# Folding a gate through Wo: column quarters of 32 with 512 columns moving, placed between two batches' query transposes

## The chip, the cores and the metric

The kernel runs on one core of a Trainium2 chip. The metric is the device time of one execution in microseconds, as the median of several runs. All tensors are fp32.

## The reference, cut to what matters

Two layers, each x + FFN(cond(x)), for x of 8 x 256 tokens and 512 features. Layer 0's cond is attention over a paged key-value cache with a window of 256; its FFN routes each token to 2 of 8 experts by a gate. What the change touches is the end of attention and the gate:

```python
o = o.transpose(0, 2, 1, 3).reshape(Bx, Tx, H * HD)
return jnp.einsum('bto,do->btd', o, Wo)          # output of attention
...
logits = jnp.clip(xt @ gate_w.T, -50.0, 50.0)    # xt: that output, gate_w: 8 x 512
top_w, top_idx = jax.lax.top_k(logits, TOP_K)
```

The logits are o Wo^T gate_w^T. The kernel therefore computes the product Wo^T gate_w^T (512 x 8) once, calls it gwo, and multiplies each batch's o by it, so that the routing need not wait for the attention's output rows.

## The kernel before, in words

The program is one long list that a scheduler puts in order on each engine: it follows the order of the code, its own estimate of times, and the buffers of the pools. Only `in_a_row` and `keep_in_program_order` fix an order by hand. [...]

Stages around the change:

- *Projection* (`with proj:`). 16 row blocks of 128 tokens get their keys and values (`keys_values`), which are written to kv_new in DRAM. Beside it, `base_weights` spreads the base weight of layer 0's FFN into delta_d, and `sum_same` and `add_delta` add sparse updates to it by indirect DMA from the GpSimd queue (six of them, BESIDE, in this stage). `gather_new(0)` gathers the new keys and values of batch 0 from kv_new on the same queue. `later(woT, ...)` and `later(gw, ...)` load Wo^T and the gate on the SP queue at row block 8.
- *Queries of batches 0 and 1*, in the same stage: for each batch `query_rows` (PE: pq, four matmuls for each 128 rows; DVE: rotation into qr; ACT: squares) and then `queries_turned` (PE: four transposes pt for each row block; ACT: copy to QT). The PSUM pools are psq and psd, three buffers each, and pw0 and pw1 are two more banks of psd.
- *The fold.* After `proj` is closed, and ahead of `prepared(0, ...)` in the code, woT is transposed in four column blocks (pw), copied by ACT to won, and for each block four matmuls with won as the stationary side and the gate's 8 columns moving add to four accumulators pgo in PSUM; four ACT copies put them in gwo. It uses the PSUM pools ps_s and ps_o, which attention uses afterwards.
- *Attention*, over batches b and halves t of 128 queries: `prepared` turns the keys of the next batch (PE: pk; DVE: KT, posb, mask), `queries(b + 2)` projects queries two batches ahead (pq from xb), `attend` makes the scores (PE: ps), masks them and takes their maximum (DVE: s<-ps,mask), exponentiates (ACT), transposes (PE: pp) and multiplies with the values (PE: po). `find_rows` (DVE: t, which, m, win, has, old) finds the rows that a later batch gathers. `gate_rows` uses gwo at the end of each batch; it is the first reader of gwo.

Of the kernel before, what the change touches and what calls it, by code (L numbers as in the profile page):

```python
# [11 lines left out]
F32 = mybir.dt.float32  # L12
I32 = mybir.dt.int32
AF = mybir.ActivationFunctionType
ALU = mybir.AluOpType
AX = mybir.AxisListType
# [3 lines left out]
P = 128  # L20
B, T, D = 8, 256, 512
# [3 lines left out]
KC = D // P  # L25
# [6 lines left out]
E = 8  # L32
# [50 lines left out]
def two_layer_kernel(ctx: ExitStack, tc: tile.TileContext, io: dict, out: bass.AP):  # L83
    nc = tc.nc
# [14 lines left out]
    ident = const.tile([P, P], F32, name="ident")  # L99
# [4 lines left out]
    RK, BW = 16, 32  # L104
# [3 lines left out]
    def in_a_row(products):  # L108

        for j, product in enumerate(products):  # L110
            if j == 0:
                product()
            else:
                with tc.high_priority():
                    tc.keep_in_program_order(product())

# [400 lines left out]
    def multiplied(py, xT, weights, experts):  # L519

        if len(experts) == 1:
            for k in range(KC):
                nc.tensor.matmul(  # L523
                    py,
                    xT[:, k, :],
                    of_expert(experts[0])(weights(k)),
                    start=(k == 0),
                    stop=(k == KC - 1),
                )
            return  # L530
        in_a_row(
            lambda k=k, h=h: nc.tensor.matmul(  # L532
                py[h * HR : (h + 1) * HR, :],
                xT[:, k, h * HR : (h + 1) * HR],
                of_expert(experts[h])(weights(k)),
                start=(k == 0),
                stop=(k == KC - 1),
            )
            for k in range(KC)
            for h in (1, 0)  # L540
        )
# [34 lines left out]
    woT = op.tile([P, KC, D], F32, name="woT")  # L576
    gwo = op.tile([P, KC, E], F32, name="gwo")
# [44 lines left out]
    with ExitStack() as att:  # L622
        ap = att.enter_context(tc.tile_pool(name="ap", bufs=1))
# [14 lines left out]
        blocks = [  # L638
            dp.tile([P, KC, 512], F32, name=f"xb{j}", tag="xb", bufs=2) for j in range(NTB + 1)
        ]  # L640
        minus_half = ap.tile([P, 1], F32, name="minus_half")
        nc.gpsimd.memset(minus_half, -0.5)

        gw = ap.tile([P, KC, E], F32, name="gw")
        epss = ap.tile([P, 2], F32, name="epss")
        nc.gpsimd.memset(epss[:, 0:1], EPS)
        nc.gpsimd.memset(epss[:, 1:2], EPS / (SCALE * SCALE))
# [380 lines left out]
        def gather_new(b):  # L1028

            gather(b, kv_new, idx_new, N)  # L1030
# [37 lines left out]
        def query_rows(i, xcols, psum, tag, pool, early=False):  # L1068

            pq = psum.tile([P, H * HD], F32, name="pq", tag=tag)  # L1070
            for k in range(KC):
                nc.tensor.matmul(  # L1072
                    pq, xcols[:, k, :], wq[:, k, :], start=(k == 0), stop=(k == KC - 1)
                )
            q3 = pq.rearrange("p (h d) -> p h d", d=HD)
            qr = pool.tile([P, H, HD], F32, name="qr")
            rotated(i, H, q3, qcos, qsin, qr, pool)
            ms = squares(q3, H, pool)
            by, eps = 1.0 / (HD * SCALE * SCALE), epss[:, 1:2]
            if early:  # L1080
                nc.scalar.activation(ms, ms, AF.Sqrt, bias=eps, scale=by)
                nc.vector.reciprocal(roots[:, i, :], ms)
            else:
                nc.vector.tensor_scalar(ms, ms, by, eps, ALU.mult, ALU.add)
                nc.gpsimd.tensor_tensor(
                    roots[:, i, :], ms, minus_half.to_broadcast([P, H]), ALU.pow
                )
            return qr

        def queries_turned(qrs, psum, tag):  # L1090

            QT = qtp.tile([P, KC, T], F32, name="QT")
            for t, qr in enumerate(qrs):
                qflat = qr.rearrange("p h d -> p (h d)")
                pt = psum.tile([P, KC, P], F32, name="pt", tag=tag)
                for m in range(KC):
                    nc.tensor.transpose(
                        pt[:, m, :], qflat[:, m * P : (m + 1) * P], ident
                    )
                nc.scalar.copy(QT[:, :, t * P : (t + 1) * P], pt)  # L1100
            return QT
# [21 lines left out]
        with proj:  # L1123
# [3 lines left out]
            psd = proj.enter_context(tc.tile_pool(name="psd", bufs=3, space=PSUM))  # L1127
# [52 lines left out]
            for i in range(LEAD):  # L1180
# [11 lines left out]
            pw = [  # L1192
                psd.tile([P, 2, NSQ, E], F32, name=f"pw{h}", tag=f"pw{h}", bufs=1)
                for h in range(2)
            ]
            for j in range(2):
                for k in range(NSQ):
                    for h in range(2):
                        rows = slice(h * ATOMS, (h + 1) * ATOMS)
# [4 lines left out]
                            start=True,  # L1204
                            stop=True,
# [77 lines left out]
            def later(tile, src, rs):  # L1283

                nc.scalar.copy(tile[:, 0, :1], rs[:, :1])
                nc.sync.dma_start(tile, src)

            FIRST = 8
            summed = placed = 0
            for i in range(LEAD, NT):  # L1290
                rs = keys_values(i)
                if i == LEAD:
                    with_gains(qcos, qsin, "q_scale")
                    rot.close()
                base_weights(i)
                if i == 3:
                    later(wq, wsrc[:, :, :512], rs)
                if i == 8:
                    later(woT, io["woT"].rearrange("(c p) o -> p c o", p=P), rs)
                    later(gw, io["gate0T"].rearrange("(c p) e -> p c e", p=P), rs)  # L1300
                if i == 4:
                    find_blocks(psd, rs)
                if i in (6, 8, 10):
                    find_rows(i // 2 - 3)
                if i in (9, 11):
                    gather_old(i // 2 - 4)
                for k in range(summed, min(summed + 3, NSC)):
                    sum_same(k)
                    summed = k + 1
                if summed - placed >= 8 or i == NT - 1:  # L1310
                    find_places(range(placed, summed))
                    placed = summed
                if i >= FIRST and i - FIRST < BESIDE:
                    add_delta(i - FIRST, sums[:, i - FIRST, :])
            gather_new(0)

            qq = proj.enter_context(tc.tile_pool(name="qq", bufs=2, side="right"))
            QTs = {}
            for b in range(2):
                rows = [  # L1320
                    query_rows(
                        i, blocks[NTB][:, :, i * P : (i + 1) * P], psq, "pkv", qq, early=True
                    )
                    for i in range(2 * b, 2 * b + 2)
                ]
                QTs[b] = queries_turned(rows, psd, "psd")


        otp = ost.enter_context(tc.tile_pool(name="otp", bufs=1, side="right"))
# [5 lines left out]
        ps_s = att.enter_context(tc.tile_pool(name="ps_s", bufs=2, space=PSUM))  # L1335
        ps_p = att.enter_context(tc.tile_pool(name="ps_p", bufs=2, space=PSUM))
        ps_o = att.enter_context(tc.tile_pool(name="ps_o", bufs=2, space=PSUM))
# [38 lines left out]
        def attend(b, t, kvs, QT, KT, mask, beside):  # L1376
            oT = oTs[b]
            for m in range(KC):
                u = m // 2

                ps = ps_s.tile([P, 2, 512], F32, name="ps")
                pss = [ps[:, r, :WU] for r in range(2)]
                in_a_row(
                    lambda r=r: nc.tensor.matmul(  # L1384
                        pss[r],
# [38 lines left out]
                for r in range(2):  # L1424
# [3 lines left out]
                    for c in range(3):  # L1428
# [6 lines left out]
                po = ps_o.tile([P, P], F32, name="po", tag="misc")  # L1435
                v0 = G * HD + 2 * u * HD
                in_a_row(
                    lambda c=c, r=r: nc.tensor.matmul(  # L1438
                        po[r * HD : (r + 1) * HD, :],
# [22 lines left out]
            nc.vector.tensor_scalar(lg0[:, i, :], pg, 50.0, -50.0, ALU.min, ALU.max)  # L1462

        AHEAD = 2

        with ExitStack() as fold:
            fo = fold.enter_context(tc.tile_pool(name="fo", bufs=1))
            pgos = [ps_s.tile([P, 2, 512], F32, name="pgo", tag="ps") for j in range(KC // 2)]
            pgo = [pgos[k // 2][:, k % 2, :E] for k in range(KC)]
            for d in range(KC):  # L1470
                pw = ps_o.tile([P, KC, P], F32, name="pw", tag="misc")
                for k in range(KC):
                    nc.tensor.transpose(pw[:, k, :], woT[:, k, d * P : (d + 1) * P], ident)
                won = fo.tile([P, D], F32, name="won")
                nc.scalar.copy(won, pw.rearrange("p c r -> p (c r)"))
                for k in range(KC):
                    nc.tensor.matmul(
                        pgo[k],
                        won[:, k * P : (k + 1) * P],
                        gw[:, d, :],  # L1480
                        start=(d == 0),
                        stop=(d == KC - 1),
                    )
            for k in range(KC):
                nc.scalar.copy(gwo[:, k, :], pgo[k])

        gather_new(1)
        ready = prepared(0, kv_rows[0])
        zero = wop.tile([P, D], F32, name="zero")
# [289 lines left out]
    with ExitStack() as cond:  # L1779
# [3 lines left out]
        with tc.tile_pool(name="ps_g", bufs=1, space=PSUM) as ps_g:  # L1783
            gwc = xab.tile([P, KC, E], F32, name="gwc", bufs=1)
            banks = [(ps_t, "pt"), (ps_g, "misc"), (ps_l, "route_a"), (ps_l, "route_b")]
# [304 lines left out]
```

## Time and profile before

| | us |
|---|---|
| median of 3 runs | 991.62 |
| lowest and highest run | 988.88, 998.61 |
| the profiled execution, as timed | 993.23 |
| its span in the profile | 991.5 |
| fold on PE (first pw to last pgo) | 107.6 to 119.1 |
| first scores on PE (ps) | 129.26 |

The page gives busy times by engine: PE is TensorE's matmuls, PEld its weight loads, DVE VectorE, ACT ScalarE, POOL GpSimd, SP the queue that issues most loads. PEclk is the clock that TensorE was granted as a share of the full one. Matmuls overlap, so the busy time of PE also holds their latency: the pitch of a group is its total time less one latency over its number less one. An fp32 matmul leaves two records, a transpose leaves one. A row of the timeline shows the start, the time, the engine, the line, what is written from what, the number of records, and in brackets the idle time before and what ended it.

### The profile page before, as it was taken

The page shows a single profiled execution, that of the slowest core. Times are in us where ns is not written, and L with a number is a line of the kernel's source. Part 1 is how long each engine was busy: PE and PEld are TensorE (multiplying, and loading weights), DVE is VectorE, ACT ScalarE, POOL GpSimd, SP SyncE. Part 2 cuts the span into 40 slices and gives each one's busy share as a digit, 9 for nine tenths or more (in the row PEclk, how much of TensorE's full clock was granted, in tenths as well). Part 3 has the DMA queues.
Part 4 walks back from the last instruction along what each step waited for, and adds up shares of the span by engine and source line. Part 5 has one row for each costly group of instructions (what it writes and reads, how often), then busy time and mean ns, then how long its engine had stood idle before and what let it go on. Part 6 is the DMA issues. An engine that isn't in the chain of part 4 may idle for free. (4 is left out here: it accounts for less than half of the span.)

```text
span 991.5 us, 14493 instructions
## 1 busy us (share of the span) xinstructions
PE 924.4 (93%) x4917; PEld 524.8 (53%) x4917; DVE 451.3 (46%) x1479; ACT 371.7 (37%) x958; POOL 356.8 (36%) x332
## 2 busy tenths in 40 slices
PE   6999889999999998897999997999599999999995
PEld 3555645556556465564433335545287777753332
DVE  5788698855846766472211112371012322323332
ACT  3676256646647589531111112410111111113221
POOL 2631646565364100305666640000223333333211
PEclk9899699999999999798999995899799999999998
DMA  6697493332432112528997655881434344333222
GB/s 190 224 315 255 133 317 107 99 97 66 138 75 76 43 44 65 190 78 310 338 258 134 127 87 160 305 311 53 170 66 73 64 76 74 64 74 63 51 29 32
DMA packets 74245, 134.71 MB, mean 136 GB/s; under 512 B 17309, under 2 KB 22941, under 8 KB 74032
## 3 DMA queue, kind: packets, MB, share of 16 engines
q0 software_dynamic: 25088, 43.68, 22.6%
q1 hardware_dynamic: 38496, 74.57, 21.7%
q10 hardware_dynamic: 10576, 15.39, 4.2%
q8 instruction: 44, 0.72, 0.3%
q14 instruction: 41, 0.34, 0.1%
HBM read 89.95 MB, written 52.56 MB: 144 GB/s over the span
## 5 line engine op out<-in xcount | busy, mean ns | idle before, releaser
L509 POOL DMA_INDIRECT xs<-g_d,token_i_l x34 | 35.2, 1035 | 241.7 <-PE pa L545 125.8
L551 DVE COPY xsT<-pa 128x512 f32<-128x512 f32 x68 | 46.8, 689 | 154.9 <-PE pa L545 150.0
L1982 DVE TENSOR_TENSOR y<-py,b 64x512 f32<-64x512 f32 (+1 forms) x46 | 31.7, 690 | 185.9 <-PE py L523 122.2
L1966 ACT ACTIVATE hs<-pu,b 128x64 f32<-128x64 f32 (+1 forms) x184 | 46.0, 347 | 186.6 <-PE pu L1940 145.2
L532 PE MATMUL py<-delta,xsT 128*64 128x512 f32 (+1 forms) x416 | 94.8, 599 | 0.0
L1415 ACT ACTIVATE s<-s,mx,roots 128x384 f32<-128x384 f32 x128 | 89.7, 704 | 12.2 <-DVE mx L1411 11.3
L1940 PE MATMUL pu<-xsT,w 128*128 128x128 f32 x704 | 84.1, 279 | 0.0
L1940 PEld LDWEIGHTS pu<-xsT,w 128*128 128x128 f32 x704 | 82.2, 196 | 0.4 <-issue 0.4
L523 PE MATMUL py<-w,hs 128*128 128x512 f32 x176 | 79.3, 594 | 0.0
L556 POOL DMA_INDIRECT out<-y,token_i_l x34 | 53.9, 1586 | 55.7 <-DVE y L1983 55.4
L1438 PE MATMUL po<-pT,kv 128*64 128x128 f32 x768 | 66.7, 285 | 7.1 <-ACT pT L1433 7.1
L1134 PE MATMUL pkv<-wkv,xb 128*128 128x512 f32 x128 | 64.6, 630 | 8.6 <-DMA wkv<-wqkvT 8.3
L1399 DVE CUSTOM_DVE_ANT_0 s<-ps,mask 128x384 f32<-128x384 f32 x128 | 67.2, 551 | 11.5 <-PE ps L1384 10.0
L1757 ACT ACTIVATE y<-py,weight_l 128x512 f32<-128x512 f32 x34 | 23.4, 687 | 125.0 <-PE py L532 89.8
L1438 PEld LDWEIGHTS po<-pT,kv 128*64 128x64 f32 x768 | 46.6, 137 | 42.9 <-ACT pT L1433 35.6
L556 POOL DMA_INDIRECT sums_d<-y,token_i_l x34 | 53.9, 1585 | 32.4 <-ACT y L1757 13.5
L1429 PE MATMUL pp<-ident,s 128*128 128x128 f32 x384 | 59.5, 282 | 3.1 <-DVE s L1426 3.1
L1384 PE MATMUL ps<-KT,QT 64*128 64x384 f32 x256 | 58.1, 533 | 4.3 <-DVE mx L1399 4.2
L1433 ACT COPY pT<-pp 128x384 f32<-128x384 f32 x128 | 55.8, 477 | 16.0 <-PE pp L1429 15.1
L545 PEld LDWEIGHTS pa<-ident,xs 128*128 128x128 f32 x272 | 32.7, 145 | 52.5 <-issue 45.9
L610 PE MATMUL ph<-woT,oT 128*128 128x512 f32 x128 | 60.3, 621 | 0.3 <-DVE lg L1462 0.3
L1072 PE MATMUL pq<-wq,xb 128*128 128x512 f32 x128 | 60.1, 618 | 0.0
(381 smaller groups left out, 1549.7 us busy)
## 6 DMA issues: line engine op xcount, KB each, us to landing
delta_d<-spread SPq DMA_DIRECT2D x16, 512.0 KB, 4.4
raw<-delta_d SPq DMA_DIRECT2D x16, 512.0 KB, 4.6
w<-fc_w SPq DMA_DIRECT2D x8, 1024.0 KB, 20.5
w<-fc_w SPq DMA_DIRECT2D x16, 512.0 KB, 14.3
part<-sums_d SPq DMA_DIRECT2D x32, 256.0 KB, 5.0
xb<-xT SPq DMA_DIRECT2D x5, 1024.0 KB, 6.3
sums_d<-zero SPq DMA_DIRECT2D x18, 256.0 KB, 4.6
kv_new<-kvt ACTq DMA_DIRECT2D x16, 256.0 KB, 3.6
```

The costliest lines, as they stand in the source:

```text
L523: nc.tensor.matmul(py, xT[:, k, :], of_expert(experts[0])(weights(k)), start=(k == 0), stop=(k == KC - 1),)
L532: lambda k=k, h=h: nc.tensor.matmul(py[h * HR : (h + 1) * HR, :], xT[:, k, h * HR : (h + 1) * HR], of_expert(experts[h])(weights(k)), star ...
L556: nc.gpsimd.indirect_dma_start(out=sum_d, out_offset=bass.IndirectOffsetOnAxis(ap=token_i[:, s : s + 1], axis=0), in_=y, in_offset=None, b ...
L610: nc.tensor.matmul(ph, oTs[i // 2][:, k, (i % 2) * P : (i % 2 + 1) * P], woT[:, k, :], start=(k == 0), stop=(k == KC - 1),)
L1072: nc.tensor.matmul(pq, xcols[:, k, :], wq[:, k, :], start=(k == 0), stop=(k == KC - 1))
L1134: nc.tensor.matmul(pkv, xb[:, k, cols], wkv[:, k, :], start=(k == 0), stop=(k == KC - 1),)
L1384: lambda r=r: nc.tensor.matmul(pss[r], QT[r * HD : (r + 1) * HD, m, t * P : (t + 1) * P], KT[r * HD : (r + 1) * HD, u, t * P : t * P + WU] ...
L1399: nc.vector.tensor_tensor_reduce(out=s, in0=pss[r], in1=mask[:, t, :], scale=1.0, scalar=NEG, op0=ALU.add, op1=ALU.max, accum_out=mx[:, r ...
L1415: nc.scalar.activation(ss[r], ss[r], AF.Exp, bias=mx[:, r : r + 1], scale=root[:, r : r + 1], accum_out=sm[:, r : r + 1],)
L1429: nc.tensor.transpose(pp[:, c * P : (c + 1) * P], s[:, c * P : (c + 1) * P], ident)
L1438: lambda c=c, r=r: nc.tensor.matmul(po[r * HD : (r + 1) * HD, :], kvs[t + c][:, v0 + r * HD : v0 + (r + 1) * HD], pTs[r][:, c * P : (c + 1 ...
L1940: nc.tensor.matmul(pu[:, c, :], w1[:, k, plan.full[s], c * P : (c + 1) * P], xsT[:, k, :], start=(k == 0), stop=(k == KC - 1),)
```

## The change

The fold moves into the projection stage, between the query rows of batch 1 and their transposes. It becomes the function `seen_through`. The gate is kept in a tile of 32 columns for each block of 128 rows of Wo's output side, cleared at first, with the 8 gate columns loaded into it. For each of the four blocks o, the block of Wo is transposed into wn (128 x 512) as before. One matmul then has the 32 gate columns as its stationary side and the 512 columns of wn moving, and writes partitions 32 o to 32 o + 31 of one accumulator acc (128 x 512). ACT copies acc to parts, four transposes turn it, and one VectorE reduce adds the four quarters (stride 32) and keeps 8 columns: gwo. The transposes use the psd pool, acc the bank of pw0.

```diff
+    def seen_through(dst, blocks, gate, pool, banks, copy, **tags):
+        acc = banks("acc", [P, D])
+        for o in range(KC):
+            pw = banks("pw", [P, KC, P])
+            for k, src in enumerate(blocks(o)):
+                nc.tensor.transpose(pw[:, k, :], src, ident)
+            wn = pool.tile([P, D], F32, name="wn", **tags)
+            copy(wn, pw.rearrange("p c r -> p (c r)"))
+            nc.tensor.matmul(
+                acc[o * BW : (o + 1) * BW, :], gate[:, o, :], wn, start=True, stop=True
+            )
+        parts = pool.tile([P, D], F32, name="parts", **tags)
+        nc.scalar.copy(parts, acc)
+        pt = banks("pt", [P, KC, P])
+        for d in range(KC):
+            nc.tensor.transpose(pt[:, d, :], parts[:, d * P : (d + 1) * P], ident)
+        nc.vector.tensor_reduce(
+            dst,
+            pt.rearrange("p d (o c) -> p d c o", o=KC)[:, :, :E, :],
+            AX.X,
+            ALU.add,
+        )
...
-        gw = ap.tile([P, KC, E], F32, name="gw")
+        gw = ap.tile([P, KC, BW], F32, name="gw")
+        nc.gpsimd.memset(gw, 0.0)
...
-                nc.sync.dma_start(tile, src)
+                nc.sync.dma_start(tile[:, :, : src.shape[-1]], src)
...
-            QTs = {}
+            QTs, rows = {}, {}
             for b in range(2):
-                rows = [
+                rows[b] = [
                     query_rows(
                         i, blocks[NTB][:, :, i * P : (i + 1) * P], psq, "pkv", qq, early=True
                     )
                     for i in range(2 * b, 2 * b + 2)
                 ]
-                QTs[b] = queries_turned(rows, psd, "psd")
+                if b == 0:
+                    QTs[b] = queries_turned(rows[b], psd, "psd")
+
+            seen_through(
+                gwo,
+                lambda o: [woT[:, k, o * P : (o + 1) * P] for k in range(KC)],
+                gw,
+                qq,
+                lambda name, shape: psd.tile(
+                    shape, F32, name=name, tag="pw0" if name == "acc" else "psd",
+                    bufs=1 if name == "acc" else 3,
+                ),
+                nc.scalar.copy,
+            )
+            QTs[1] = queries_turned(rows[1], psd, "psd")
...
-        with ExitStack() as fold:
-            fo = fold.enter_context(tc.tile_pool(name="fo", bufs=1))
-            pgos = [ps_s.tile([P, 2, 512], F32, name="pgo", tag="ps") for j in range(KC // 2)]
-            pgo = [pgos[k // 2][:, k % 2, :E] for k in range(KC)]
-            for d in range(KC):
-                pw = ps_o.tile([P, KC, P], F32, name="pw", tag="misc")
-                for k in range(KC):
-                    nc.tensor.transpose(pw[:, k, :], woT[:, k, d * P : (d + 1) * P], ident)
-                won = fo.tile([P, D], F32, name="won")
-                nc.scalar.copy(won, pw.rearrange("p c r -> p (c r)"))
-                for k in range(KC):
-                    nc.tensor.matmul(
-                        pgo[k],
-                        won[:, k * P : (k + 1) * P],
-                        gw[:, d, :],
-                        start=(d == 0),
-                        stop=(d == KC - 1),
-                    )
-            for k in range(KC):
-                nc.scalar.copy(gwo[:, k, :], pgo[k])
```

## The prediction

> **What bounds the kernel now.** I read the page first: the busy shares, then the row of granted clocks, because a TensorE (PE) that is 93% busy may still be slow in places.
>
> ```profile
> PE 924.4 (93%) x4917; PEld 524.8 (53%) x4917; DVE 451.3 (46%) x1479; ACT 371.7 (37%) x958; POOL 356.8 (36%) x332
> ...
> PEclk9899699999999999798999995899799999999998
> ```
>
> PE sets the time in most stages, so what counts is PE's time, or what makes PE wait, in the stage that is changed. A slice of the clock row is 24.8 us; the fifth one (99 to 124 us) shows 6, and the fold lies there. I then asked for the tile pgo, which the removed code writes:
>
> ```profile
> L1477 PEld LDWEIGHTS pgo<-gw,won x32: 289/334/338, 109.4 to 118.7; 128*128 128x128 f32 x32
> L1477 PE MATMUL pgo<-gw,won x32: 361/362/383, 109.4 to 118.8; 128*128 128x8 f32 x32
> ...
>   ACT won L1475: 6.1, 3
> ```
>
> One fp32 matmul leaves two records, so 16 matmuls are 32 records. Each of them loads 128 columns (334 ns) to move only 8; PE pays for loads here. Next the table of windows of that stretch (columns: us, busy time of PE, PEld, DVE, ACT, POOL, granted clock, DMA share, GB/s):
>
> ```profile
> 100.00:105.00 5.00, 4.22 (x16) 2.02 (x13) 4.71 (x14) 2.29 (x5) 2.76 (x2) 1.00 0.12 2
> 105.00:110.00 5.00, 3.01 (x15) 2.53 (x15) 4.99 (x12) 1.97 (x4) 4.00 (x3) 0.77 1.00 319
> 110.00:115.00 5.00, 5.00 (x25) 4.63 (x24) 1.03 (x4) 1.17 (x2) 2.92 (x3) 0.50 0.41 111
> 115.00:120.00 5.00, 5.00 (x25) 4.82 (x25) 0.85 (x2) 1.05 (x5) 4.09 (x5) 0.50 0.30 60
> 120.00:125.00 5.00, 5.00 (x8) 2.01 (x7) 3.90 (x14) 0.00 (x0) 3.92 (x5) 0.52 0.78 256
> 125.00:130.00 5.00, 5.00 (x15) 2.09 (x15) 3.98 (x10) 0.60 (x1) 2.80 (x4) 1.00 1.01 321
> ```
>
> VectorE (DVE) has almost nothing to do from 110 to 120 us, while PE runs the fold at half clock. The timeline shows what stands before and behind it:
>
> ```profile
> 106.31 0.63 PE L1097 MATMUL pt<-ident,qr 128*128 128x128 f32 x4 [2.09 <-DVE qr L1066]
> 107.62 1.94 PE L1473 MATMUL pw<-ident,woT 128*128 128x128 f32 x8 [0.68 <-ACT QT L1100]
> 110.10 1.00 POOL L1034 DMA_INDIRECT kv<-kv_new,idx_new  x1 [0.30 <-issue]
> 118.98 1.09 PE L1354 MATMUL pk<-ident,kv 128*128 128x128 f32 x4
> 119.87 9.46 PE L1072 MATMUL pq<-wq,xb 128*128 128x512 f32 x16
> 129.26 1.56 PE L1384 MATMUL ps<-KT,QT 64*128 64x384 f32 x8
> 130.64 0.55 DVE L1399 CUSTOM_DVE_ANT_0 s<-ps,mask 128x384 f32<-128x384 f32 x1
> ```
>
> PE stands still for 2.1 us (DVE is turning the query rows), then for 0.7, then folds until 119.1, with the first key transposes (pk) between, and only then finishes pk, the projection of batch 2's queries (pq) and the first scores (ps). The first score is masked by DVE at 130.64: attention starts there. I use this time as the mark.
>
> [...] the clock went from 1.00 to 0.50 at about 107.7, after the gap from 104.2 to 106.3, and returned at about 124.7, [...] in the dense pq. [...] (po with 64 columns 137 ns on average, pq with 128 columns 191), so the new load of 32 gate columns should be cheap. [...] The new matmul is 128x32 among 128x128 transposes; for the nearest mix before (po, 128*64, between pp, 128*128) the timeline has idle times of 0.17 us at the load. Three groups of such matmuls give some 1 us at most.
>
> **The change, part by part.**
>
> *Removed.* 16 matmuls on 8 columns (32 records x 0.23 us pitch, 1.88 us for 8: 7.5 us), 16 transposes of Wo (two groups of 0.97 inside the first 1.94 us, then two of 1.09: 4.1 us), four copies won (0.59 us each) and four copies to gwo. As they stand at half clock, fold and pk fill PE from 107.62 to 119.87, 12.25 us, of which pk is 2.2. The 16 transposes come back as they were, at full clock 0.11 us each (four take 0.60 with 0.28 of latency): 1.8 us.
>
> *Added.* Four matmuls with 512 columns moving: 8 records at the pitch of pq (12 in 5.40 us: 0.44) are 3.5 us at full clock. Bounds: not below 3.5, [...]; 7.0 at half clock. I take 3.5. One ACT copy parts (128x512 from PSUM, 0.59), four transposes (0.60), one VectorE reduce of 128 elements (the reduces of 256 and 512 took 0.41 and 0.68, so about 0.28 on that line; 0.2 to 0.5 allowed for its stride). The clearing of gw on GpSimd, 128 elements against 0.55 us for 512, is about 0.2 us in the first microseconds, when PE waits for the first loads: nothing, at most 0.2.
>
> *Moved.* In the changed order PE goes from the last pq (ends about 103.7) straight into ten transposes of Wo, two of the new matmuls, six transposes, two matmuls, then parts, then the eight transposes of qr. Step by step: pw0 done 104.2; ACT copies wn 104.25 to 104.83 and to 105.42, in the place of the old QT copy; acc 104.9 to 106.6; the other six transposes to 107.5; wn copies (behind sq, which ends 105.8) 107.0 to 108.2; acc 107.65 to 109.5; parts to 110.15; its transposes to 110.8; those of qr to 111.7; the QT copies on ACT to 112.5. So QT1 is ready 5 us later than before (107.6), and nobody misses it, as pk comes later.
>
> *Queues.* woT was issued at 72.5 and landed 11.4 us later, gw at 82.9 and 4.4, so the wait for them costs nothing. The loads of xb and xin on SP still wait for the last pq, so they go at the same time. On GpSimd nothing is moved: the four gathers of kv_new for batch 0 stand among the scatters into delta_d, each of which waits for the landing of the one before (3.7 us apart). The last gather is issued at 110.10 and landed 3.4 us later, 113.5. Before, this was covered by the fold. Now it is what is late next: PE waits 113.5 − 112.5 = 1 us more for it. On DVE, the reduce into gwo stands ahead of posb, mask and the KT copies and waits until 110.8; DVE has that slack (1.03 us busy in 110 to 115).
>
> *From 113.5 on.* pk at 113.5, KT copies 114.1 to 115.5 (0.69 each), pq from 114.85: at full clock 16 x 0.43 = 6.9, to 121.8; if the clock falls in the gap before pk, [...]. But DVE decides: after the KT copies its own list up to xrot is 3.9 us (mask, held, two m, entries, two posb, win, has, t), to 119.4; then xrot, qr, rs and the small ones of the first row block, 4.5 us, to 123.9; then xrot and qr of the second, 1.4. So the first score is masked at 125.3, not 130.64: 5.3 us earlier. The new order leaves 0.3 us more of DVE's small work (which, two m, less posb and the reduce) for later: 5.0.
>
> *Given back.* PE has its first scores done by 123.3 to 124.9 and must wait until about 127.8 (DVE puts qr and rs between the second and the first mask; before, that gap was 2.1 us, from 130.8 to 132.9). A gap of 3 to 4.4 us is about as long as what brought the clock down at 107.7. Then the opening of attention runs at half clock [...]; there PE is busy for 6.19 of 10 us (130 to 140), [...]. With about 0.7 chance: 1 us.
>
> Sum: 5.0 − 1.0 = 4.0 us. From there on PE is full (20.0 of 20 us in 140 to 160) and its work is the same, so I let the gain run to the end. The profiled execution took 993.23 us (span 991.5), 1.6 more than the median of 991.62; the same gain on each gives 989.2 and **987.6 us**.
>
> **Rivals.**
> 1. *PE, not DVE, carries the start of attention, and the clock stays up.* Then the gain is that of the ps row, 129.26 − 121.8 = 7.5 us, to some 10 if later low-clock spells (404, 453, 600 and 709 us) also fall better: 984 to 981. For it: PE full from 139 on. Against: DVE 9.84 of 10 us in 130 to 140.
> 2. *The gain is hidden.* Should the new matmuls run at half clock (7.0 us), QT1 is ready at about 116 and the first score at about 128: 2.8 less 0.3 and the 1 us given back leave 1.5; and if the gathers land 2 us later as well, nothing: 990 to 992. For it: the fold's half clock until now. Against: no gap ahead of the fold any more.
> 3. *Slower: the clock.* The longer gap at 123 to 128 drops the clock, and the opening of attention, with narrow transposes, doesn't bring it back. [...]: 3.5 us slower, 995; [...]. For it: the fold and its transposes never brought it back. Against: ps moves 384 columns, and the spell at 709 ended with matmuls on 128 columns, at 722.
>
> **How the numbers follow.** My forecast has 0.55 (its own range 985 to 990.5), rival 1 0.17, rival 2 0.18, rival 3 0.10. The runs before spread from 988.88 to 998.61, so 1% is about what a measurement can tell. Below 981.7 (faster by over 1%) lies most of rival 1 at its best and a tail of mine: 0.16. Over 1001.5 lies the end of rival 3: 0.05. The rest, 0.79, is within 1%. The range goes from 981, near the end of rival 1, to 994.5, into rival 3.
>
> **What would show it right or wrong.** Right: PE without a gap between 103.7 and 106.5 and a clock of 1.00 there; the acc rows with a pitch of 0.43 us; PE waiting for the kv gather just before pk; pk at about 113.5; the first mask (s<-ps) at about 125. Wrong: acc at 0.86; pk late because of QT or parts; DVE idle before the first mask (then PE was the bound); PEclk of 0.5 beyond 135; or an end of attention that isn't earlier by what its start gained.

## The result, and the profile after

| | us |
|---|---|
| after, median of 20 runs (lowest, highest) | 996.32 (991.45, 1000.8) |
| before, median of 20 runs on the same chip | 992.83 |
| after / before, with 95% interval | 1.0037 [1.0019, 1.0055] |
| after, the profiled execution and its span | 995.66, 993.9 |

The kernel became slower by 3.5 us in the medians (0.37%), where 4 us less were forecast. The ratios in this document leave out single executions in a slower state, such as one of 1192 us in e5, while the medians include them. The page of the changed kernel hardly tells the two apart: PE has 2.7 us less to do, and in the clock row the fifth slice (99 to 124 us) stands at 8 for 6 before, the sixth at 8 for 9.

```profile
PE 921.7 (93%) x4897; PEld 517.4 (52%) x4897; DVE 453.5 (46%) x1478; ACT 372.7 (37%) x957; POOL 355.9 (36%) x333
...
PEclk9799889999999999798999996899899999999998
```

The timeline of PE in the changed kernel, from the last pq of the projection stage to the first scores (start, time, what, records, and in brackets the idle time before and what ended it):

```profile
102.91 2.74 PE L1098 MATMUL pq<-wq,xb 128*128 128x512 f32 x6
105.49 1.25 PE L124 MATMUL pw<-ident,woT 128*128 128x128 f32 x10
106.77 1.53 PE L127 MATMUL acc<-wn,gw 128*32 128x512 f32 x4
108.23 0.87 PE L124 MATMUL pw<-ident,woT 128*128 128x128 f32 x6
109.40 1.53 PE L127 MATMUL acc<-wn,gw 128*32 128x512 f32 x4 [0.29 <-ACT wn L126]
...
112.10 1.04 PE L1123 MATMUL pt<-ident,qr 128*128 128x128 f32 x8
113.86 0.33 PE L1394 MATMUL pk<-ident,kv 128*128 128x128 f32 x1 [0.73 <-DVE posb L1401]
118.25 0.47 PE L1394 MATMUL pk<-ident,kv 128*128 128x128 f32 x1 [4.05 <-DMA kv<-kv_new,idx_new]
120.44 0.47 PE L1394 MATMUL pk<-ident,kv 128*128 128x128 f32 x1 [1.72 <-DMA kv<-kv_new,idx_new]
121.92 1.33 PE L1394 MATMUL pk<-ident,kv 128*128 128x128 f32 x5 [1.01 <-DMA kv<-kv_new,idx_new]
123.25 9.00 PE L1098 MATMUL pq<-wq,xb 128*128 128x512 f32 x16
132.18 1.56 PE L1424 MATMUL ps<-KT,QT 64*128 64x384 f32 x8
```

Down to 113 us this is the change as it was meant: the fold runs into the last pq without a gap, at full clock, and with the transposes of qr it is over at 113.1. Then the reader should follow the brackets: PE waits for a gather three times, 4.05 + 1.72 + 1.01 = 6.8 us in sum. Before, pk had not waited at all. The windows of the changed kernel (columns as in the prediction's) show what comes with that:

```profile
114.00:118.00 4.00, 0.19 (x1) 0.00 (x0) 0.60 (x2) 0.00 (x0) 3.39 (x3) 0.85 0.14 9
118.00:122.00 4.00, 1.03 (x3) 0.45 (x4) 0.00 (x0) 0.00 (x0) 3.08 (x4) 0.50 0.56 131
122.00:126.00 4.00, 4.00 (x9) 2.05 (x10) 3.41 (x9) 0.00 (x0) 3.09 (x4) 0.50 0.14 18
```

From 114 to 122 us PE works for 1.2 us, DVE for 0.6 and ACT not at all; only GpSimd is at work. The clock falls to 0.85 and then to 0.50, and the pq behind it takes 9.00 us. The same 16 records take 7.13 us in runs below that have them at full clock (e6, e10: a pitch of 0.44), so the low clock costs nearly 2 us there. This can't all be put down to the wait: before, pq took 9.46 us, and in e1 below, where PE waits for no gather, it takes 8.56. The gathers stand in GpSimd's queue, which in the changed kernel reads:

```profile
94.76 1.66 POOL L1131 DMA_INDIRECT delta_d<-sums,put_i  x1 [18.60 <-DMA kv_new<-kvt]
98.62 1.86 POOL L1131 DMA_INDIRECT delta_d<-sums,put_i  x1 [2.20 <-ACT rs L1173]
104.53 1.55 POOL L1131 DMA_INDIRECT delta_d<-sums,put_i  x1 [4.05 <-ACT sq L1072]
109.30 1.55 POOL L1131 DMA_INDIRECT delta_d<-sums,put_i  x1 [3.22 <-issue]
...
118.36 1.00 POOL L1060 DMA_INDIRECT kv<-kv_new,idx_new  x1 [0.30 <-issue]
```

Five scatters into delta_d stand ahead of the last gather, each waiting for the landing of the one before: the first three land 3.1, 5.2 and 4.0 us after they go out, and the next one goes out 0.7 to 0.8 us after each landing. The last gather goes out at 118.36, where it went out at 110.10 before, though the last pq ended only 1.9 us later.

### The profile page after: what moved, and what is told of

Same layout as the page of the kernel before. It is cut to its first block, busy times and chain, and to the rows that moved or that the text cites. A ratio compares the mean times of both kernels' runs of the same rounds, so it can differ in the third digit from the quotient of the medians.

```text
span 993.9 us, 14459 instructions
## 1 busy us (share of the span) xinstructions
PE 921.7 (93%) x4897; PEld 517.4 (52%) x4897; DVE 453.5 (46%) x1478; ACT 372.7 (37%) x957; POOL 355.9 (36%) x333
## 5 line engine op out<-in xcount | busy, mean ns | idle before, releaser
L1455 ACT ACTIVATE s<-s,mx,roots 128x384 f32<-128x384 f32 x128 | 89.7, 705 | 11.2 <-DVE mx L1451 10.1
L570 PE MATMUL pa<-ident,xs 128*128 128x128 f32 x272 | 43.9, 287 | 16.6 <-DMA xs<-g_d,token_i_l 11.2
```

What stands on the lines that cost most here:

```text
L570: nc.tensor.transpose(dst[:, k, :], src[:, k * P : (k + 1) * P], ident)
L1455: nc.scalar.activation(ss[r], ss[r], AF.Exp, bias=mx[:, r : r + 1], scale=root[:, r : r + 1], accum_out=sm[:, r : r + 1],)
```

## The experiments

The last pq of the projection stage ends anywhere from 101.6 to 109.4 us in these profiles: at 103.8 and 103.9 in the two executions of the kernel before, but at 107.1 in e2, which differs from it only later. So stages are compared from the end of that pq, and totals by the medians and ratios. My theory was that the gathers of batch 0 decide now, since the old fold had covered them; rivals were the clock, the form of the fold, and the clearing of gw.

**The gathers issued early, in the changed kernel (e1) and in the one before (e2).** With BESIDE at 2 only two scatters stand ahead of the gathers; the other four follow in attention.

```diff
-        BESIDE = 6
+        BESIDE = 2
```

> The changed kernel with two scatters into delta_d (not six) ahead of batch 0's gathers on the GpSimd queue; the other four join the groups beside attention. Theory G (the gathers of kv_new, queued behind scatters that each wait for the landing of the one before, set the start of attention now that the old fold no longer covers them): the last gather is issued at about 108 to 109 instead of 118.4 us, pk ends its wait by about 113 instead of 121.9, the first mask comes at 125 to 127 instead of 133.8, and the run is 6 to 8 us below the changed kernel, 2 to 4 us below the kernel before (ratio 0.996 to 0.998). Theory O (the other order of the projection stage makes everything 2 to 4 us late by itself, whatever the gathers do): the first mask moves by less than 2 us, ratio 1.002 to 1.004. Theory C (the clock: after gaps PE runs at half clock in pq and in the opening of attention): half the gain, ratio about 1.000, with a clock of 0.5 still in pq or behind 135 us.

> The control: the same edit (two scatters ahead of the gathers, not six) in the kernel before. Theory G: the old fold covers the gathers there, so the first mask stays at 130 to 131 us and the ratio is 1.000 within 0.001; perhaps a little slower where the four scatters now stand in attention. If the edit gains by itself, whatever the fold (a rival to G): ratio 0.996 to 0.998 here too.

Measured: e1 987.66 us, ratio to before 0.9949 [0.993, 0.9967], 0.9% under the changed kernel; e2 992.2, 0.9986 [0.9963, 1.0008], which can't be told from no change. The timeline of PE in e1, and DVE's first mask:

```profile
110.41 1.04 PE L1123 MATMUL pt<-ident,qr 128*128 128x128 f32 x8
112.17 1.18 PE L1394 MATMUL pk<-ident,kv 128*128 128x128 f32 x8 [0.73 <-issue]
114.86 8.56 PE L1098 MATMUL pq<-wq,xb 128*128 128x512 f32 x16 [1.51 <-DVE KT L1397]
123.35 1.56 PE L1424 MATMUL ps<-KT,QT 64*128 64x384 f32 x8
124.98 0.55 DVE L1439 CUSTOM_DVE_ANT_0 s<-ps,mask 128x384 f32<-128x384 f32 x1
```

The waits for gathers are gone: pk follows the transposes of qr, and the first mask comes 21.0 us after the last pq (124.98 − 103.96), against 28.2 in the changed kernel (133.81 − 105.65) and 26.9 before. From there to the last gate row (the last lg<-pg on DVE) e1 and the changed kernel take about the same (280.0 and 279.8 us), so the gain lies where the wait was. It is larger than expected for e1 (0.996 to 0.998), and about what was forecast for the change. In e2 the first mask comes 24.9 us after the last pq, 2.0 earlier than before, but the total shows no gain clear of noise: as far as can be measured, the old fold had been covering the gathers.

**The clearing of gw, moved late in the changed kernel (e3), and put alone into the kernel before (e4).** In e3 the memset stands right ahead of gw's load at row block 8. In e4 nothing of the fold changes but the width of gw's tile, with the slices that keep to its 8 columns, and its clearing at the program's start.

```diff
 # e3, on the changed kernel
-        nc.gpsimd.memset(gw, 0.0)          # at the start
...
+                    nc.gpsimd.memset(gw, 0.0)   # at i == 8
                     later(gw, ...)
 # e4, on the kernel before
-        gw = ap.tile([P, KC, E], F32, name="gw")
+        gw = ap.tile([P, KC, BW], F32, name="gw")
+        nc.gpsimd.memset(gw, 0.0)
```

> The changed kernel with one statement moved: gw is cleared just ahead of its load instead of at the top. In the built program the scheduler then gives the projection stage the order of the kernel before on ScalarE (the last spread ahead of two kvt copies). Theory G with the order as its cause: the last spread goes out at about 86.5 instead of 90.6 us, the first scatter starts at about 90 instead of 94.8, the last gather at 110 to 112 instead of 118.4, the first mask at 125.5 to 128; 4 to 6 us below the changed kernel, ratio 0.997 to 0.999. If the lateness of the chain was only that one execution's (the order makes no difference): ratio 1.003 to 1.004 as for the changed kernel, with a first scatter anywhere from 90 to 95. Theory C: ratio about 1.001.

> The kernel before with only the wider gw and its clearing at the top (the fold as it was, reading the 8 columns). The built program then has the order of the changed kernel in the projection stage. If that order is what delays the chain: the first scatter at about 94 to 95 us, the last gather landing at 119 to 122, so that the old fold no longer covers it fully; the first mask 1 to 4 us later than 130.6, ratio 1.001 to 1.004. If the order makes no difference: 1.000 within 0.001.

Measured: e3 993.42 us, ratio 0.9999 [0.9981, 1.0018]; e4 996.3, 1.0028 [1.0007, 1.0049]. So the early clearing costs about 0.3 to 0.4% in either kernel; for e3 0.997 to 0.999 had been expected. It is not its own time: it takes 0.20 us, at 0.99 us from the start. What differs is the scheduler's order of the projection stage. ScalarE's last copy of a base weight (spread) is the witness; the first scatter goes out 4.7 to 5.2 us after it in every profile. First before, then the changed kernel, each with the last write of kv_new behind it:

```profile
85.44 1.04 ACT L1167 COPY spread<-w 128x1024 f32<-128x1024 f32 x1
...
97.20 0.33 ACTq L1151 DMA_DIRECT2D kv_new<-kvt  x1
```

```profile
89.58 1.03 ACT L1193 COPY spread<-w 128x1024 f32<-128x1024 f32 x1
...
99.27 0.33 ACTq L1177 DMA_DIRECT2D kv_new<-kvt  x1
```

The last write follows the last spread by 11.8 us in the kernel before and by 9.7 in the changed one: the scatters start some 2 us later in the stage. The others agree with their clearing, not with their fold: 12.2 in e3, 10.0 in e4, and over all thirteen profiles 9.6 to 10.1 with the early clearing, 11.0 to 12.2 without. The third scatter then comes later still: in e4 it follows the second by 5.8 us, in the changed kernel by 5.9.

```profile
96.84 1.56 POOL L1106 DMA_INDIRECT delta_d<-sums,put_i  x1 [2.12 <-ACT rs L1148]
102.61 1.59 POOL L1106 DMA_INDIRECT delta_d<-sums,put_i  x1 [4.21 <-ACT QT L1101]
```

In e3 these are 3.99 us apart (97.19, 101.18), the last gather goes out at 113.13, PE waits 0.60 us for a gather, the clock stays up, and the first mask comes 19.2 us after the last pq: 7.6 earlier than before. The total still does not beat before. Half of the 7.6 us is lost in attention: from the first mask to the last gate row e3 takes 281.9 us, where before took 278.1 (279.7 in its second execution, e8). The rest is missing ahead of it, where e3's last pq ended at 107.5; with one profile of e3 I can't say whether that belongs to the version or to the execution.

**Both together (e5).** e3 with BESIDE at 2.

> The changed kernel with both edits: gw cleared late (the projection stage in the order of before) and two scatters ahead of batch 0's gathers. Theory G: with the gathers early, the order of the projection stage matters little for them, as they then wait for the last write of kv_new only; first mask at 124 to 125.5 us and 986 to 989 (ratio 0.993 to 0.997), about like the same kernel with the early clearing (987.66, 0.9949). Theory A (attention itself became 2 to 4 us longer by the scheduler's other order, as in the late-clearing run, where mask to last gate row took 281.6 us against 277.7 before): the first mask at 124.5, but 990 to 992. If the early order costs 3 us by itself: 983 to 985.

Measured: 988.01 us, ratio 0.9919 [0.9891, 0.9947], the lowest ratio of all. Its interval overlaps that of e1, and its median without the run of 1192 us, 987.65, is no lower than e1's 987.66. So it is not shown that the two gains add up. Against e3, which differs from it in BESIDE alone, the gain is clear, but a wait taken from PE doesn't explain it: PE had waited only 0.60 us in e3. In the one profile of each the first mask comes 18.4 us after the last pq (e3: 19.2), and attention takes 279.2 us (281.9); but e5's profiled execution, with 992.02 us, lies 4 us above its median. What the early gathers gain in this kernel is open.

**Form and place apart, gathers early.** e6 has the new form (32 gate columns stationary, 512 columns moving) at the old place after the projection stage, with the late clearing. e7 has the old form (blocks of Wo stationary, 8 gate columns moving) at the new place, with a gw of 8 columns and no clearing.

```diff
 # e6: at the old place
+            seen_through(gwo, lambda o: [...], gw, fo, bank, nc.scalar.copy, tag="fo")
 # e7: between the query rows of batch 1 and their transposes
+            pgo = psd.tile([P, KC, E], F32, name="pgo", tag="pw0", bufs=1)
...
+                won = qq.tile([P, D], F32, name="won", bufs=KC)
+                nc.scalar.copy(won, pw.rearrange("p c r -> p (c r)"))
...
+            nc.scalar.copy(gwo, pgo)
+            QTs[1] = queries_turned(rows[1], psd, "psd")
```

> Only the new form of the fold (32 gate columns stationary, 512 moving, one accumulator, parts turned and reduced) in the fold's old place, with one staging buffer, two scatters ahead of the gathers, gw cleared late. If the form is what gains (the old fold's loads): PE needs 3 to 4 us less, first mask at 127.5 to 129, ratio 0.995 to 0.997. If the place gains (PE has no gap ahead of the fold, the clock stays up, QT1's turn is hidden): the chain pw, copy, acc, copy, transposes, reduce is as long as the old fold there (about 9 us), first mask at 131 to 133, ratio 0.998 to 1.001.

> Only the new place: the old form (gate's 8 columns moving, won stationary, 16 matmuls) between batch 1's query rows and their transposes, its four sums in one bank, four staging buffers; two scatters ahead of the gathers. If the place gains: at full clock the 32 records take 4.2 us (eight took 1.06 where the clock was up) against 3.5 for the new form, so first mask at 124.5 to 126.5 and ratio 0.993 to 0.997, like the changed kernel with early gathers. If the form gains: first mask at 128 or later, ratio 0.998 to 1.001.

Measured: e6 997.27 us, ratio 1.0042 [1.0019, 1.0064]; e7 985.92, 0.9932 [0.9904, 0.9961]. The place gains and the form, as built in e6, doesn't; e6 is slower than either branch of its expectation. The timeline of PE in e7:

```profile
104.64 3.07 PE L1365 MATMUL pgo<-gw,won 128*128 128x8 f32 x26
107.98 0.90 PE L1401 MATMUL pk<-ident,kv 128*128 128x128 f32 x3 [0.28 <-ACT gwo L1372]
109.72 1.33 PE L1401 MATMUL pk<-ident,kv 128*128 128x128 f32 x5 [0.83 <-DMA kv<-kv_new,idx_new]
```

At full clock 26 records of the old form take 3.07 us, 0.12 us each, where they had 0.23 in the old fold at half clock. All 32 are then about 3.8 us, where the new form's eight records take 3.06 (two groups of 1.53). What made the old form look dear was the clock at its old place.

**The same two with all six scatters (e9, e10), and the changed kernel again (e11).** e9 is e7 and e10 is e6, each with BESIDE back at 6. The expectations speak of six scatters ahead of the gathers; the queue shows five, the sixth follows.

> The old form of the fold (block of Wo stationary, 8 gate columns moving) at the new place, no clearing of gw, six scatters into delta_d ahead of batch 0's gathers as before: e7 without the early gathers. Theory (the place makes PE free early and the gathers then decide): PE waits some 4 to 8 us for the last gather, which lands at 113 to 118 us; first mask 26 to 28 us after the last pq of the stage instead of e7's 19.7; ratio 0.997 to 1.001. Rival (the old form at the new place is what makes e7 fast, whatever the gathers do): ratio 0.991 to 0.995, no wait of over 1.5 us for a gather ahead of pk.

> The new form of the fold (32 gate columns stationary, 512 columns moving) at the old place, gw cleared late, six scatters as before. Theory (the form by itself is worth little where the fold stands at half clock): first mask 24 to 27 us after the last pq, ratio 0.998 to 1.004, any loss lying in attention's longer steps and not ahead of the first mask. Rival (the narrow form saves its 4 us to the end): ratio 0.994 to 0.996.

> The changed kernel once more, for its marks. Theory (six scatters and gathers in a chain, in the order that the early clearing gives): second to third scatter again over 5 us apart, last gather of batch 0 issued 10 us or more after the last pq of the stage, PE waiting for gathers ahead of pk for 5 us or more in sum, first mask 26 to 30 us after the last pq. Rival (the late gathers were an accident of that one execution): scatters 3.7 to 4.0 us apart, last gather within 7 us of the last pq, first mask 20 to 23 us after it.

e9 measured 992.83 us, 0.9987 [0.9971, 1.0002], and its timeline of PE shows the same wait with the other form, 3.29 us the longest of four that sum to 6.6:

```profile
114.03 0.47 PE L1401 MATMUL pk<-ident,kv 128*128 128x128 f32 x1 [3.29 <-DMA kv<-kv_new,idx_new]
116.01 0.47 PE L1401 MATMUL pk<-ident,kv 128*128 128x128 f32 x1 [1.51 <-DMA kv<-kv_new,idx_new]
117.43 1.33 PE L1401 MATMUL pk<-ident,kv 128*128 128x128 f32 x5 [0.94 <-DMA kv<-kv_new,idx_new]
```

Its first mask comes 26.1 us after the last pq, where it came after 19.7 in e7, and attention takes the same in both (279.6 and 279.2 us). Again the gain of the early gathers lies where the wait was.

e10 measured 996.12 us, 1.0036 [1.0008, 1.0064]. Its first mask comes 24.8 us after the last pq, 2.1 earlier than before, but from there to the last gate row it takes 282.9 us, 4.8 more than before (3.2 more than e8). e6 is alike: 22.5 us, then 282.5. Two of PE's costliest groups between the first gate row of batch 0 and that of batch 2 (159.6 to 236.5 us before, 156.6 to 239.3 in e10), first in the kernel before, then in e10; after the bar come busy time, mean ns and idle time ahead:

```profile
L1438 PE MATMUL po<-pT,kv 128*64 128x128 f32 x192 | 15.7, 282 | 0.0
...
L1384 PE MATMUL ps<-KT,QT 64*128 64x384 f32 x60 | 13.5, 531 | 0.8 <-DVE mx L1399 0.8
```

```profile
L1467 PE MATMUL po<-pT,kv 128*64 128x128 f32 x192 | 16.7, 283 | 1.7 <-ACT pT L1462 1.7
...
L1413 PE MATMUL ps<-KT,QT 64*128 64x384 f32 x68 | 15.3, 532 | 1.9 <-DVE mx L1428 1.7
```

In e10 PE waits 3.6 us for ACT and DVE there, against 0.8 before, and eight more records of ps fall into that stretch. That stretch is 5.8 us longer. So attention's instructions came out in another order, which loses more than the fold had gained. The three profiles with attention over 281 us (e3, e6, e10) all have the late clearing, so at the old place no run tells the new form from the clearing that came with it; e5, which has it too, took 279.2.

e11, one run of 998.29 us, repeats the changed kernel's marks: the third scatter 6.1 us after the second (97.38, 103.47), the last gather at 117.73, three waits for gathers of 6.8 us in sum, the first mask 27.6 us after the last pq (132.59 − 105.02). The late gathers were no accident of one execution.

**The kernel before once more (e8).**

> The kernel before once more, for one profile, since the marks of single executions vary. Theory G expects the first scatter at 90 to 93.5 us and, with the old fold covering the gathers, the first mask at 130 to 132.5 whatever the scatters do. If the first profile's early chain (90.2) was typical of this order, 90 to 91 again.

Measured: 994.14 us in its one run, with the first mask 27.5 us after the last pq. Here the fourth scatter, out at 103.72, met the loads of xb and xin, which SP issues as the last pq ends (104.0 to 105.5). The fifth left only at 110.63, where it left at 105.18 in the profile of before, and even the old fold did not quite cover the gathers: pk waited 1.1 us for them.

Ratios to before, in one view:

| fold | scatters: 6 | scatters: 2 |
|---|---|---|
| old form, old place | 1 | 0.9986 |
| old form, old place, early clearing (e4) | 1.0028 | |
| new form, old place, late clearing | 1.0036 | 1.0042 |
| old form, new place | 0.9987 | 0.9932 |
| new form, new place, late clearing | 0.9999 | 0.9919 |
| new form, new place, early clearing (the change) | 1.0037 | 0.9949 |

The intervals of the two forms at the new place overlap in either column. Three versions beat both kernels, all with early gathers at the new place.

## Why the prediction was wrong

*Right in kind: the fold's own cost.* PE has no gap between 103.7 and 106.5, measured from the last pq; the clock there is full; the two records of one matmul start 0.45 us apart, near the 0.43 forecast. The sum for acc was still too high, 3.06 us for 3.5 that were called a lower bound, since one matmul runs into the next (last section). Of the 32-column load the prediction said only that it should be cheap: it takes 106 to 110 ns, against 334 in the old fold at half clock and 192 for the same 128 columns at full clock (e7). The queries of batch 1 are turned 7.5 us after the last pq for a forecast of 8.0, and the reduce took 0.29 us for a forecast of 0.28.

*Wrong, and the step that failed:* "On GpSimd nothing is moved: the four gathers of kv_new for batch 0 stand among the scatters into delta_d". It had seen the chain, named the gathers as what is late next, and then carried over the old time of the last gather, 110.10, as if it were fixed. It is not: the chain takes as long as its landings (2.9 to 6.8 us each, last section), and it starts when ScalarE has spread the last base weight. The gather went out at 118.36 and was read at 121.92, so PE waited 6.8 us where the sum had 1. e1 against e2 shows that to issue the gathers early is worth 0.9% in the changed kernel and nothing that can be measured in the one before; e7 against e9 shows the like with the other form (0.55%).

*Wrong: the clearing of gw at nothing.* Its 0.2 us was the right size. The cost lies elsewhere, in the order that the scheduler gave to a stage 80 us later: 0.28% when added alone (e4), 0.38% when taken back (e3). The term was left out, not mis-sized. In the three profiles with six scatters and the early clearing the last gather goes out 18.8 to 19.1 us after the last write of kv_new. In those with six scatters and without it the time is 12.2 (e3), 12.9 (before), 16.2 (e10), 17.3 (e9) and 18.0 (e8, the same program as before): in e3 and before the fifth scatter left 3.6 and 3.9 us after the fourth, and in the other three, where the first load of xb was issued within 1.4 us of the fourth (before: 2.6 us), 5.4 to 6.9 us after it. So the gathers were late in all three profiles with the early clearing and in some without; and since PE waits as long in e9 (6.6 us) as in the changed kernel (6.8), the 0.5% between these two is not all in the gathers. I can't place the rest.

*Wrong: the first mask at 125.3.* It came at 133.81. That "DVE decides" was half right:

```profile
128.85 0.76 DVE L1083 TENSOR_TENSOR xrot<-pq,qsin 128x256 f32<-128x256 f32 x2 [1.67 <-PE pq L1098]
...
133.81 0.54 DVE L1439 CUSTOM_DVE_ANT_0 s<-ps,mask 128x384 f32<-128x384 f32 x1
```

From xrot to the mask DVE works without a gap, 4.96 us for the 5.9 forecast, and PE's first scores are done just in time (133.74). But ahead of xrot DVE stands idle for 1.67 us, waiting for the late pq. In e3, where the clock stays up, it has no such wait from the KT copies to the mask (117.30 to 126.74). With the gathers early (e1) the mask comes 21.0 us after the last pq, 5.8 earlier than before; forecast were 5.0, with 1 us of waiting for a gather in it.

*Right in kind: the clock.* The prediction gave 0.7 to a spell at half clock in the opening of attention, for 1 us; the length of the spell behind that 1 us was its author's estimate. A spell came earlier, in the gap ahead of pk, which the prediction had as a branch; pq paid 1.9 us for it (9.00 against 7.13), and in e9 it took 9.2. A short dip stands where the forecast had it (0.66 in the window from 138 to 142). The third rival, in which the clock alone makes the kernel slower (995 us, an estimate: a spell as long as that from 107.7 to 124.7 loses half of its 17.0 us, 8.5, against 5.0 gained), is not what happened: with the gathers early pq still takes 8.56 us (e1) and 8.81 (e7), and both are faster than before. The windows of e1 show that the fall needs no long wait (the clock is the number after POOL):

```profile
112.00:114.00 2.00, 1.18 (x8) 0.84 (x8) 0.90 (x3) 0.12 (x1) 1.83 (x3) 1.00 0.61 172
114.00:116.00 2.00, 1.14 (x2) 0.63 (x3) 1.89 (x5) 0.00 (x0) 1.69 (x2) 0.59 0.90 318
```

PE had worked for more than half of these two windows, and its longest gap was 1.51 us. In e3 and e5 the clock stays at 1.00 up to the end of pq with PE as busy (1.03 of 2 us from 116 to 118 in e3). What decides between the two is not shown. In the trace before the clock had fallen behind gaps of 2.09 and 0.68 us, and a busy PE did not soon bring it back: its windows are full from 110 to 120 us at a clock of 0.50, and 1.00 stands again in the window from 125 to 130.

*Wrong in part: "its work is the same, so I let the gain run to the end".* It holds for e9 and the changed kernel, which take 279.6 and 279.8 us from the first mask to the last gate row, as before did (278.1, and 279.7 in e8). It does not hold for e3, where attention took 2.2 to 3.8 us more, nor for e10. Of the rivals the second (the gathers land later and the gain is hidden) had the mechanism; it counted on 2 us and on no loss beyond zero.

*Open.* Why one edit of a tile changes the order of attention; what the early gathers gain in e5 over e3; and what makes up the 4.8 us in e10 and the 3.8 in e3, measured from the first profile of before: in e10 PE's waits between the two gate rows are 2.8 us more than before, and no run was made to take them away.

## What to carry to other kernels

When work that stood ahead of a wait is moved or shortened, the time at which that wait ends has to be worked out anew from its own chain: each landing, each queue place, and what starts it. A number from the old trace is only the time that used to be hidden. Where a scheduler orders the program, no edit is free for being small; ask what order each one gives, and run the small edits alone. And a form that looks dear at half clock should be priced at full clock before it is replaced: here the old form, only moved, did as well as the new one.

## What the runs showed of the hardware that was not expected

- Most scatters into delta_d whose landing is on record land after 2.9 to 4.0 us. Three that met the loads of xb and xin took 5.8 to 6.8 (102.91 in e9, 103.72 in e8, 105.18 before), and the chain stretches with them: in e8 the fifth scatter left 6.9 us after the fourth, before 3.9. Two took 5.2 and 5.4 with a write of kv_new issued up to 1.3 us behind them (98.62 in the changed kernel, 97.38 in e11). But two others with such a write close behind took 3.2 and 3.4 (94.73 in e10, 94.24 in e9), so the write alone does not explain it.
- Matmuls of 32 stationary columns that wrote different partition quarters overlapped. In the changed kernel the third record of acc, the first of the second matmul, starts some 0.03 us after the second one (107.25, 107.22); its windows, of acc alone (span, PE busy and records, PEld, ACT, clock, DMA share, GB/s), show three of four records begun within 0.63 us, though each takes about 0.6. The two matmuls take 1.53 us together, where four records of pq take 1.88:

```profile
106.77:107.40 0.63, 0.63 (x3) 0.27 (x4) 0.00 (x0) 1.00 1.19 44
...
106.70:108.30 1.60, 1.53 (x4) 0.27 (x4) 0.00 (x0) 1.00 1.01 150
```

- A record of a 128x8 matmul took 0.12 us at full clock (26 in 3.07 us, e7) and 0.23 at half (8 in 1.88 us, before), with a load of 128 columns for each (0.192 and 0.334 us). With 512 columns moving the pitch of pq is 0.44, so it did not follow the columns down to eight.
- Loads of 32 columns took 0.106 to 0.110 us (acc in the changed kernel), not a quarter of what 128 columns took (pq: 0.190 in the median), and loads of 64 columns 0.137 in the mean (po): fewer columns took less time, but not in proportion.
